# Moving weight-block loads, factors and stores to other steps of the first four attention jobs

## The chip, the cores and the metric

One core of a Trainium2 chip. The metric is the device time in microseconds of one execution; lower is better. TensorE (PE in the profile) does the matmuls, ScalarE (ACT) exponentials and copies, VectorE (DVE) sums and reductions. SyncE (SP) issues most DMAs, GpSimd (POOL) issues the accumulating ones.

## The reference

Two attention layers over x of shape (8, 512, 32, 32), fp32. For each batch element and layer, with S = 1024 positions, C = 512 channels and 8 heads of 64:

```python
xn  = groupnorm(x, 8 groups) * gamma + beta
q, k, v = Wq xn + bq, Wk xn + bk, Wv xn + bv        # 512 x 512 weights
out = softmax(q^T k / 8) v                          # per head, over 1024 positions
x   = x + Wp out + bp
```

## The kernel before, in words

The 16 pairs of batch element and layer are jobs, numbered n = 0 to 15 and ordered so that two batch elements go through layer 0 (jobs 0 and 1) and then through layer 1 (jobs 2 and 3), and so on. For each job TensorE runs the projections and then the attention.

**Projections** are done by Strassen-like recipes with seven products in place of eight. They need sums of weight blocks ("factors"). One level of this needs the seven sums of a whole matrix (S1 to S4 beside the raw blocks); two levels need seven such sets, 49 small blocks, stored as seven tiles of 128 x 7 x 128. The weights are the same for all batch elements, so the sums are made once, in jobs 0 to 3, and kept in DRAM: `keep` (one level) or `deep_...` tiles. Later jobs fetch these with `fetch()` (line 181) into a ring of six tiles; the profile names the transfer w<-deep.

The sums are made on VectorE in the attention of the early jobs, beside TensorE's work, by two helpers:

- `put_round(which, layer)` makes all 49 blocks of one matrix ("a round" or batch): a load of four raw blocks (round<-wp_dram or round<-wqkv_dram, 256 KB each), eight chores of VectorE (`first` and `second`, lines 165 to 171, four of 128x512 and four of 128x896), and seven stores of 448 KB (deep<-round). Jobs 0 to 3 do the output matrix of layer 0, V of layer 1, output of layer 1, V of layer 0.
- `put_first(which, layer)`, in jobs 0 and 1 only, makes the one-level factors of K and of Q of layer 1: a load (raw<-wqkv_dram, four of 256 KB), four chores (128x512), and a store in two DMAs, 768 and 256 KB (keep<-raw).

Both take the same SBUF buffer, tag "deep", of which there is one. The inner sums of the next job's activations (`deep_steps`, lines 485 to 491) are written to it as well. Each user waits until the one before is stored or read. In job 0 the order is round, raw, deep; in job 1 raw, round, deep; in jobs 2 and 3 round, deep.

**Attention** of a job is 64 steps i, in eight groups g (four head pairs by two halves of the queries). A step does the scores sc of one block of keys on TensorE, the exponential e on ScalarE (line 1107), and the product with the values (po) for step i - 2. The sums of e per query are made by VectorE (acc, lines 1121 and 1123), partly by GpSimd's accumulating DMA e<-e (line 1130) and an add of its result (line 1133). Each group ends with a take of po into q (line 1176) and a reduction of acc (line 1188, called at step 8g + 10). After an odd g the reciprocals follow: `gather` (three small DMAs r<-r, line 1211), `invert` (line 1215 on, then the DMA rd<-rt and two broadcasts back, rb<-rd, lines 1228 and 1230), `normalise` (line 1245, q times rb). Their times after the reduction are written down:

```python
times = (0.0, 12.0, 12.1, 22.0) if n in ROUNDS and g < 4 else (0.0, 7.6, 7.7, 16.2)
```

A step advances the planner's clock by 1.71, the end of a group by another 0.85. So in jobs 0 to 3 the first inversion (g = 1, reduced in step 18) comes within step 25, ahead of that step's tables, and its multiply at the end of step 30; the second (g = 3, reduced in step 34) comes within step 41, and its multiply at the end of step 46.

**Order.** PE, ACT and DVE run in the order in which the program is written. What is done beside attention stands in three tables by step, called at the end of the step in this order: `chores` (VectorE's work, at most one a step: `put` takes the next free step), `moves` (loads, stores, ScalarE's work, likewise by `move`), `leaving` (a round's stores, two per step). DMAs of `in_turn` keep their place in SP's program. SP starts them one after another, and an entry that waits holds all behind it.

In the kernel before, the tables come to these steps:

| | job 0 | job 1 | jobs 2, 3 |
|---|---|---|---|
| round: load | 6 | 12 | 9 |
| round: eight chores | 12-16, 18-20 | 16, 18, 22-27 | 13-16, 18-21 |
| round: stores | 27-30 | 28-31 | 27-30 |
| raw: load | 35 | 2 | |
| raw: four chores | 39-42 | 6, 7, 9, 10 | |
| raw: store | 43 | 11 | |
| sums of the next job's xn (t, lines 426 to 432) | 31-34 | 17, 19-21 | 31-34 |
| inner sums into "deep" | 46-49 | 37-40, 42, 44, 46, 48 | 36-38, 40, 41, 43, 45, 47 |

The groupnorm of the next job but one stands beside this: in job 1 its `groups` (DMAs dg and mr) at step 8, its coefficients at 14, its four applies on ScalarE at 15 to 18.

Of the kernel before, what the change touches and what calls it, by code (L numbers as in the profile page):

```python
# [54 lines left out]
ROUNDS = {0: (O, 0), 1: (V, 1), 2: (O, 1), 3: (V, 0)}  # L55
# [26 lines left out]
def fast_path(  # L82
# [33 lines left out]
    def later(delay, fn):  # L116
        todo.append((clock[0] + delay, fn))
# [97 lines left out]
    def deep_round(which, layer):  # L215


        box = []

        def start():  # L220
            t = acts.tile([P, NW, NW, P], F32, tag="deep", name=f"round_{which}_{layer}")
            box.append(t)
            for i in range(2):
                for j in range(2):
                    in_turn(
                        t[:, 2 * j + i, 0:4, :].rearrange("p (cc h) o -> p cc (h o)", cc=2),
                        raw_block(layer, which, i, j),
                    )

        def outer_(part):  # L230
            factor(box[0][:, :, 0:4, :], part)

        def inner(part):
            factor(box[0].rearrange("p f a o -> p a f o"), part)

        def store(o):
            keep = wdram.tile([P, NW, P], F32, name=f"deep_{which}_{layer}_{o}")
            in_turn(keep, box[0][:, FACTOR[o]])
            deep[which, layer, o] = keep

        first = [lambda part=part: outer_(part) for part in range(4)]
        second = [lambda part=part: inner(part) for part in range(4)]
        return start, first, second, [lambda o=o: store(o) for o in OUTER]
# [1186 lines left out]
    first = v_phase(0, (1, 5, 2, 6, 7, 3, 4), v0)  # L1430
# [113 lines left out]
    for n in range(-1, len(jobs)):  # L1544
        last = n + 1 == len(jobs)
        outs = None
        if n >= 0:
            chores, moves, leaving = {}, {}, {}

            def put(i, fn):  # L1550
                while i in chores:
                    i += 1
                chores[i] = fn
                return i

            def move(i, fn):
                while i in moves:
                    i += 1
                moves[i] = fn
                return i  # L1560

            def put_round(which, layer):
                load, first, second, stores = deep_round(which, layer)
                begin = {0: 6, 1: 12}.get(n, 9)
                move(begin, load)
                at = begin + 3
                for fn in first:
                    at = put(at + 1, fn)
                for fn in second:
                    at = put(at + 1, fn)  # L1570
                at = max(at, 26)
                for i in range(4):
                    leaving[at + 1 + i] = lambda part=stores[2 * i : 2 * i + 2]: [fn() for fn in part]

            def put_first(which, layer):
                at = move(35 if n == 0 else 2, lambda: start()) + 3
                box = []

                def start():
                    box.append(acts.tile([P, NW, 2, CH], F32, tag="deep", name=f"raw_{n}"))  # L1580
                    load_blocks(box[0], layer, which)

                for part in range(4):
                    at = put(at + 1, lambda part=part: factor(box[0], part))
                move(at + 1, lambda: store_factors(box[0], layer, which))

            if last:
                w = last_weights(n)
                for part in range(4):
                    put(12 + 2 * part, lambda part=part: factor(w, part))  # L1590
                for i, fn in enumerate(last_sums(0)):
                    put(49 + 3 * i, fn)
            else:
                for i, (_, fn) in enumerate(extra):
                    put(2 + i, fn)
                if n == 1:
                    at = (8, 14, 15, 16, 17, 18, 17, 19, 20, 21)
                else:
                    for i, fn in zip((3, 3, 4, 5, 5, 6, 7, 7, 8), reads):
                        put(i, fn)  # L1600
                    at = (16, 22, 23, 24, 26, 27, 29, 31, 33, 35)
                    if n < DEEP_V + 2:
                        at = (17, 24, 26, 27, 29, 30, 31, 32, 33, 34)
                for i, fn in zip(at[:2], steps):
                    put(i, fn)
                for i, fn in zip(at[2:], steps[2:]):
                    move(i, fn)
                if n == 1:
                    put_first(*FIRST[n])
                for i, fn in zip(at[len(steps) :], sums(n + 1)):  # L1610
                    put(i, fn)
                if n in ROUNDS:
                    put_round(*ROUNDS[n])
                if n == 0:
                    put_first(*FIRST[n])
                put(52 if n in ROUNDS else 48, lambda q=att.q: out_combine(q, None, 0))
                deep_first = deep_steps(n + 1)
                if n + 1 >= DEEP_V:
                    for i, fn in enumerate(deep_first):
                        put(37 + 2 * i if n not in ROUNDS else ((37, 38, 39, 40, 42, 44, 46, 48) if n == 1 else (36, 37, 38, 40, 41, 43, 45, 47))[i], fn)  # L1620
                else:
                    for at, fn in zip((46, 47, 48, 49), deep_first[4:]):
                        put(at, fn)
                move(58, lambda: extend_plan(n + 1))
                for _ in range(RING):
                    move(58, fetch)
            assert max([*chores, *moves], default=0) < NT * len(att.groups) + LEAD
            if n + 1 >= DEEP_V and not last:
                outs = OutputSums(n)
                ahead = deque()  # L1630
                if jobs[n][1] == 1 and jobs[n][0] + 2 < B:
                    ahead.extend(load_steps(jobs[n][0] + 2))
                both, plan_sums = deep_phases(n + 1, ahead, outs)

                att.run(chores, moves, leaving, True)
                extra = ahead
                plan_sums()
                banks(0, "one")
                if n + 2 < len(jobs):
                    reads, steps = norm_steps(n + 2)  # L1640
                att.take(len(att.groups) - 1, both[0])
                banks(1, "one")
                for thunk in both[1:]:
                    thunk()
                banks(0, "two")
                att = Attention(n + 1)
                att.scores(0)
                att.scores(1)
                banks(1, "two")
                att.scores(2, "po")  # L1650
                continue
            att.run(chores, moves, leaving)
            banks(0, "one")
            banks(1, "one")
            if last:
                for i, fn in enumerate(last_sums(1)):
                    later(7.1 + 0.8 * i, fn)
                later(13.0, judge)
                for sh in range(2):
                    last_proj(n, w, sh)  # L1660
                break
            outs = OutputSums(n)
            out_sums(n, outs)
            first = v_phase(n + 1, ORDER)
            for thunk in first[:-1]:
                thunk()
            rest = first[-1:]
            extra = deque()
            if jobs[n][1] == 1 and jobs[n][0] + 2 < B:
                extra.extend(load_steps(jobs[n][0] + 2))  # L1670
            if n == 0:
                load, bias_steps = make_out_bias(1)
                extra.append((8, load))
                extra.extend((11, fn) for fn in bias_steps)
            if n + 2 < len(jobs):
                reads, steps = norm_steps(n + 2)
                if n + 2 <= DEEP_V:
                    extra.extend((15, fn) for fn in reads)
        both, _ = deep_phases(n + 1, extra, outs, deep_first[:4] if outs else ())
        both[0]()  # L1680
        rest[0]()
        if n < 0:
            later(22.0, lambda: load_x(1))
        for thunk in both[1:]:
            thunk()
        banks(0, "two")
        att = Attention(n + 1)
        att.scores(0)
        att.scores(1)
        banks(1, "two")  # L1690
        att.scores(2, "po")
# [249 lines left out]
```

## Time and profile before

| | |
|---|---|
| median of 3 runs | 3171.83 us (3170.29 to 3174.29) |
| the profiled execution | 3173.06 us, span 3171.3 us |
| TensorE clock granted, mean | 0.998 |
| first scores of jobs 0, 1, 2, 3 | 78.86, 285.10, 487.48, 683.18 us |
| DMA moved | 450.31 MB, mean 142 GB/s |

Times in views are microseconds from the start of the span. In a list of waits, each line names the engine, the line and the result of the operation that waited, what it waited for, and then the total, the number of waits and the longest. A line of a timeline gives start, duration, engine, line, operation, operands and, in brackets, the idle time before it and what ended that. SPq is SP's queue of issues: its durations are those of issuing, not of moving data.

### The profile page before, as it was taken

What the parts mean: (1) busy time and instruction counts of PE and PEld (TensorE: products, weight loads), DVE (VectorE), ACT (ScalarE), POOL (GpSimd) and SP (SyncE); (2) the same over time, 40 slices, a digit from 0 to 9 for tenths busy, and PEclk for the clock granted to TensorE, in tenths of its full rate; (3) what the DMA queues carried; (4) which work ended last, traced back from release to release, by engine and by line L of the source; (5) the groups of instructions that cost most, each with busy time, mean ns of one, the idle gap of its engine ahead of it and who ended that gap; (6) DMA issues with size and microseconds to landing.
All of it is one profiled execution on the core that took longest, in us unless ns stands there. A gap on an engine that the chain in (4) does not pass through costs nothing.

```text
span 3171.3 us, 62173 instructions
## 1 busy us (share of the span) xinstructions
PE 3151.6 (99%) x24093; PEld 1874.4 (59%) x24093; DVE 2636.1 (83%) x3571; ACT 2333.4 (74%) x4233; POOL 281.1 (9%) x318
## 2 busy tenths in 40 slices
PE   9999999999999999999999999999999999999999
PEld 7356384663946639366483754837557375573844
DVE  8887898979879788896978969789697887978967
ACT  6648687786877768677686776867768687686864
POOL 0100101001010010100001000010000100001000
PEclk9999999999999999999999999999999999999999
DMA  7645575566635454455554535446456463444733
GB/s 277 149 132 164 136 225 134 145 190 153 219 75 148 109 141 137 85 163 148 141 179 95 163 91 142 120 95 188 129 138 181 89 202 62 132 126 95 223 75 82
DMA packets 186190, 450.31 MB, mean 142 GB/s; under 512 B 37928, under 2 KB 54176, under 8 KB 185888
## 3 DMA queue, kind: packets, MB, share of 16 engines
q1 hardware_dynamic: 137040, 296.82, 27.3%
q0 software_dynamic: 48848, 149.44, 25.9%
q8 instruction: 192, 3.15, 0.4%
q14 instruction: 110, 0.90, 0.1%
HBM read 247.41 MB, written 48.17 MB: 93 GB/s over the span
## 4 chain that ended last, share of the span: by engine, by line
PE 92%; DVE 4%; DMA 1%; issue 1%; SPq 0%; ACT 0%; DVEq 0%; POOL 0%; ACTq 0%; POOLq 0%
PE sc L1102 25%; PE po L1153 25%; PE vd L809 11%; PE zd L809 11%; PE yd L809 5%; PE ud L809 4%; PE vd L804 4%; PE zd L804 3%; PE ud L804 1%; PE yd L804 1%; DVE acc L1123 1%; PE z L556 1%; DVE acc L1133 1%; DMA keep<-raw 0%; DVE r L1188 0%
## 5 line engine op out<-in xcount | busy, mean ns | idle before, releaser
L1107 ACT ACTIVATE e<-sc 128x1024 f32<-128x1024 f32 x1024 | 1044.4, 1025 | 573.9 <-PE sc L1102 546.7
L1153 PE MATMUL po<-e,v 64*64 64x512 f32 x8192 | 1057.7, 589 | 2.0 <-ACT e L1107 2.0
L1102 PE MATMUL sc<-q,k 64*64 64x512 f32 x8192 | 1058.2, 589 | 0.3 <-ACT e L1107 0.2
L1153 PEld LDWEIGHTS po<-e,v 64*64 64x64 f32 x8192 | 312.9, 133 | 568.5 <-issue 541.3
L1102 PEld LDWEIGHTS sc<-q,k 64*64 64x64 f32 x8192 | 311.0, 133 | 563.7 <-issue 508.6
L1123 DVE TENSOR_TENSOR acc<-acc,e 128x1024 f32<-128x1024 f32 x320 | 389.7, 1218 | 39.3 <-ACT e L1107 28.6
L1130 POOL DMA_DIRECT2D e<-e x224 | 192.9, 861 | 1759.5 <-ACT e L1107 1297.9
L1121 DVE TENSOR_TENSOR acc<-e,e 128x1024 f32<-128x1024 f32 x128 | 156.5, 1223 | 147.6 <-ACT e L1107 147.5
L1133 DVE TENSOR_TENSOR acc<-acc,e 128x1024 f32<-128x1024 f32 x224 | 272.6, 1217 | 1.8
L809 PE MATMUL zd<-deep,w 128*128 128x256 f32 x860 | 240.1, 379 | 0.0
L809 PE MATMUL vd<-deep,w 128*128 128x256 f32 x804 | 223.5, 379 | 0.0
L809 PEld LDWEIGHTS zd<-deep,w 128*128 128x128 f32 x860 | 163.4, 190 | 22.2
L809 PEld LDWEIGHTS vd<-deep,w 128*128 128x128 f32 x804 | 152.8, 190 | 20.8
L1188 DVE TRANSPOSE_TENSOR_REDUCE r<-acc 128x32 f32<-128x1024 f32 x128 | 159.4, 1245 | 4.3
L904 POOL DMA_DIRECT2D x<-p x61 | 72.9, 1196 | 972.2 <-ACT p L826 510.3
L851 DVE TENSOR_TENSOR p<-p,s 128x512 f32<-128x512 f32 x185 | 127.5, 689 | 23.8 <-ACT p L826 19.4
L804 PE MATMUL vd<-w,deep 128*128 128x128 f32 x840 | 119.5, 276 | 1.5 <-ACT ud L504 1.5
L851 DVE TENSOR_TENSOR q<-q,s 128x512 f32<-128x512 f32 x64 | 44.2, 691 | 87.3 <-ACT q L828 45.6
L804 PEld LDWEIGHTS vd<-w,deep 128*128 128x128 f32 x840 | 106.5, 192 | 2.0 <-ACT ud L504 1.9
L804 PE MATMUL zd<-w,deep 128*128 128x128 f32 x728 | 106.9, 276 | 0.1
L809 PE MATMUL vd<-os,w 128*128 128x256 f32 x364 | 105.5, 379 | 0.0
L809 PE MATMUL zd<-os,w 128*128 128x256 f32 x356 | 98.9, 379 | 0.0
(296 smaller groups left out, 4824.6 us busy)
## 6 DMA issues: line engine op xcount, KB each, us to landing
w<-deep SPq DMA_DIRECT2D x399, 448.0 KB, 4.9
e<-e POOLq DMA_DIRECT2D x224, 512.0 KB, 4.7
x<-p POOLq DMA_DIRECT2D x61, 512.0 KB, 6.7
rb<-rd SPq DMA_DIRECT2D x96, 256.0 KB, 3.7
x<-x_dram SPq DMA_DIRECT2D x28, 512.0 KB, 5.5
out_dram<-x SPq DMA_DIRECT2D x28, 512.0 KB, 5.5
deep<-w SPq DMA_DIRECT2D x28, 448.0 KB, 5.9
deep<-round SPq DMA_DIRECT2D x28, 448.0 KB, 9.4
```

The source lines that it names most:

```text
L804: nc.tensor.matmul(ps[:, tokens], moving[i][:, tokens], lhs[:, FACTOR[i], :], start=(start and ti == 0), stop=True, skip_group_check=True,)
L809: nc.tensor.matmul(ps, lhs[:, FACTOR[i], :], moving[i], start=start, stop=True, skip_group_check=True,)
L851: nc.vector.tensor_add(to_, to_, five.to_broadcast([P, 2, QT]))
L904: nc.gpsimd.dma_start(to_, p(part), accum_op=ALU.add)
L1102: nc.tensor.matmul(sc[h * HD : (h + 1) * HD, j, :], k[r, hp, k0 : k0 + HD], q[r, hp, sh * HALF : (sh + 1) * HALF], start=True, stop=True,)
L1107: nc.scalar.activation(e, sc, AF.Exp, scale=SCALE)
L1121: nc.vector.tensor_add(acc[g], self.es[i - 1], e)
L1123: nc.vector.tensor_add(acc[g], acc[g], e)
L1130: nc.gpsimd.dma_start(self.summed[i], self.summed.pop(i - 1), accum_op=ALU.add)
L1133: nc.vector.tensor_add(self.acc[g], self.acc[g], self.summed.pop(i))
L1153: nc.tensor.matmul(po[g][j * HD : (j + 1) * HD, h, :], v[r, kc, d0 : d0 + HD], e[r, j, :], start=(kc == 0), stop=(kc == NT - 1),)
L1188: nc.vector.tensor_reduce(self.r[:, 0, m, :], self.acc.pop(g).rearrange("p j (b e) -> p (j b) e", e=RP), AX.X, ALU.add, apply_transpose=True,)
```

## The change

It moves work to other steps; no operation is added or taken out.

- Job 0: the round's stores follow its last chore. The raw blocks' load is asked for at step 29 in place of 35 (29 and 30 are taken by applies, so it comes to 31), their chores start from a fixed step, and the inner sums come two steps sooner.
- Job 1: the raw chores follow directly on the load; the round's load moves from 12 to 8, its chores stand in a row, its stores follow; the sums of xn come after them; the inner sums come two steps sooner.
- Jobs 2 and 3: the stores follow the last chore.

```diff
             def put_round(which, layer):
                 load, first, second, stores = deep_round(which, layer)
-                begin = {0: 6, 1: 12}.get(n, 9)
+                begin, at = {0: (6, 11), 1: (8, 14)}.get(n, (9, 12))
                 move(begin, load)
-                at = begin + 3
-                for fn in first:
+                for fn in first + second:
                     at = put(at + 1, fn)
-                for fn in second:
-                    at = put(at + 1, fn)
-                at = max(at, 26)
                 for i in range(4):
                     leaving[at + 1 + i] = lambda part=stores[2 * i : 2 * i + 2]: [fn() for fn in part]
 
             def put_first(which, layer):
-                at = move(35 if n == 0 else 2, lambda: start()) + 3
+                at = {0: 35, 1: 2}[n]
+                move({0: 29, 1: 2}[n], lambda: start())
                 box = []
...
                 if n == 1:
-                    at = (8, 14, 15, 16, 17, 18, 17, 19, 20, 21)
+                    at = (8, 14, 15, 16, 17, 18, 23, 24, 25, 26)
                 else:
...
-                        put(37 + 2 * i if n not in ROUNDS else ((37, 38, 39, 40, 42, 44, 46, 48) if n == 1 else (36, 37, 38, 40, 41, 43, 45, 47))[i], fn)
+                        put(37 + 2 * i if n not in ROUNDS else ((35, 36, 37, 38, 40, 42, 44, 46) if n == 1 else (36, 37, 38, 40, 41, 43, 45, 47))[i], fn)
                 else:
-                    for at, fn in zip((46, 47, 48, 49), deep_first[4:]):
+                    for at, fn in zip((44, 45, 46, 47), deep_first[4:]):
                         put(at, fn)
```

The tables after it:

| | job 0 | job 1 | jobs 2, 3 |
|---|---|---|---|
| round: load | 6 | 8 | 9 |
| round: eight chores | 12-16, 18-20 | 15-22 | 13-16, 18-21 |
| round: stores | 21-24 | 23-26 | 22-25 |
| raw: load | 31 | 2 | |
| raw: four chores | 36-39 | 3-6 | |
| raw: store | 40 | 7 | |
| sums of the next job's xn | 31-34 | 23-26 | 31-34 |
| inner sums into "deep" | 44-47 | 35-38, 40, 42, 44, 46 | 36-38, 40, 41, 43, 45, 47 |

## The prediction

> **What bounds the kernel now.** I read the page first. TensorE is busy almost without a break:
>
> ```profile
> PE 3151.6 (99%) x24093; PEld 1874.4 (59%) x24093; DVE 2636.1 (83%) x3571; ACT 2333.4 (74%) x4233; POOL 281.1 (9%) x318
> ```
>
> Only some 20 us of the 3171.3 us span are not matmul, so the question is whether the edited stages hold part of them. The edits touch attention jobs 0 to 3. Their first scores start at 78.86, 285.10, 487.48 and 683.18 us by the timeline. Second view, TensorE's waits from 79 to 485 us (engine, line and operation, what it waited for, total, times, longest):
>
> ```profile
> PE v L556 <- DVE q L1176: 3.5, 1, 3.5
> PE vd L804 <- DMA w<-deep: 2.3, 1, 2.3
> PE po L1153 <- ACT e L1107: 2.0, 2, 1.7
> PE z L556 <- DMA w<-wqkv_dram: 1.2, 1, 1.2
> PE vd L804 <- ACT ud L504: 1.1, 1, 1.1
> PE sc L1102 <- ACT e L1107: 0.2, 1, 0.2
> ```
>
> The timeline places them. Job 0 loses 1.74 at 187.5, 1.21 at 190.3 and 3.48 at 197.2: 6.43 us. Job 1 loses 0.28 at 394.5, 2.31 at 395.9, 1.1 at 415.3 and about 0.7 near 318. Later stages show next to nothing (0.42 at 807.9). Third, stretches of time (length, busy time of PE, PEld, DVE, ACT, POOL, granted clock, DMA share, GB/s):
>
> ```profile
> 200.00:204.00 4.00, 2.96 (x7) 2.43 (x8) 3.83 (x9) 0.00 (x0) 0.00 (x0) 0.57 0.84 259
> ...
> 396.00:400.00 4.00, 1.69 (x13) 1.28 (x7) 3.97 (x4) 0.59 (x1) 0.00 (x0) 0.81 1.02 365
> 400.00:404.00 4.00, 4.00 (x29) 4.00 (x29) 3.69 (x4) 2.97 (x8) 0.00 (x0) 0.76 1.02 404
> ```
>
> After each group of waits the clock falls: 4 x 0.43 = 1.72 us lost in job 0, 4 x (0.19 + 0.24) = 1.72 in job 1. The neighbours stand at 1.00.
>
> Why is TensorE late only there? The waits end on VectorE, or on weight fetches that queue behind VectorE's work. VectorE's own waits, first of 79 to 200, then of 285 to 400 us:
>
> ```profile
> DVE deep L485 <- DMA keep<-raw: 5.9, 1, 5.9
> DVE raw L165 <- DMA raw<-wqkv_dram: 4.9, 1, 4.9
> ```
>
> ```profile
> DVE deep L485 <- issue: 5.9, 1, 5.9
> ...
> DVE round L165 <- DMA round<-wqkv_dram: 5.7, 1, 5.7
> ```
>
> So VectorE stands 10.8 us in job 0 and 11.6 in job 1 for weight blocks in the one "deep" buffer. (The third, called issue, ends when the seven stores deep<-round have landed: the last was issued at 348.73.) After each stall it runs unbroken to the end of the job, so it cannot catch up. The last column sum of the attention shows the debt:
>
> ```profile
> 200.90 1.24 DVE L1188 TRANSPOSE_TENSOR_REDUCE r<-acc 128x32 f32<-128x1024 f32 x1
> ```
>
> ```profile
> 601.47 1.25 DVE L1188 TRANSPOSE_TENSOR_REDUCE r<-acc 128x32 f32<-128x1024 f32 x1
> ```
>
> The first is 122.0 us after job 0's first score, the second 114.0 after job 2's; job 1 has 120.8, job 3 114.7. Jobs 2 and 3 run without those TensorE waits, so 8.0 and 6.8 us of lateness is what has to go.
>
> Last, SP's issues (start, length of issue):
>
> ```profile
> 115.34 1.85 SPq L1211 DMA_DIRECT2D r<-r  x3
> 124.93 0.33 SPq L1228 DMA_DIRECT2D rd<-rt  x1
> 126.31 1.31 SPq L1230 DMA_DIRECT2D rb<-rd  x2
> 127.67 8.71 SPq L155 DMA_DIRECT2D deep<-round  x7
> 143.57 2.55 SPq L1211 DMA_DIRECT2D r<-r  x3
> 146.31 3.22 SPq L155 DMA_DIRECT2D raw<-wqkv_dram  x4
> ```
>
> SP issues in program order. The raw loads of job 0 stand behind the second r<-r, which waits for VectorE's reduction at 142.3; the stores stand behind rd/rb, although their data was finished at 115.9.
>
> **What the Trainium skill says.** "TensorE: Matmul & The Clock Gate", What's actually happening: an idle window of about 3.4 us halves TensorE's clock, and a busy one restores it. The trace agrees: two spells of 3.413 us at 0.5, after these two groups of waits; but job 1's 2.6 us of standing were enough for it. The same page, Architectural detail: VectorE's queue is strictly first in, first out. The trace agrees: during the 5.89 us stand, adds whose operands were ready stood behind it. "DMA: Bandwidth & Descriptors", HWDGE ordering: descriptors of one queue are taken in order, and a transfer's completion lands only after the earlier writes of the same DMA engines. So rd placed behind stores lands after them. The trace agrees in kind: rd landed 1.4 us after its issue on quiet engines (124.93), 4.8 after (157.78) with accumulations under way.
>
> **The change, part by part.** No instruction is added or removed; all durations below are of this trace. Steps are 1.717 us apart.
>
> *Job 0, stores* (steps 27-30 to 21-24). The inversion with rd/rb runs inside step 25, so all seven stores now precede it on SP. They start behind r<-r at 117.2 rather than 127.7. Issuing seven took 6.7 us in job 1 and 8.7 here, so SP is free at 124 to 126; rt is ready at 124.9, so rd slips by 0 to 1 us. Data: 448 KB per 1.12 us in the steady part, 7.8 us in all, plus 1 to 2 for the accumulation still running until about 119.5: drained at 128 to 129.5. The engines stood idle in 120:124 (share 0.02), so this cover exists. rd lands at about 129.5 rather than 126.3, rb follows at 129.5 to 131 and lands at 134 to 136 (133.6 before). VectorE waits for it at L1245: 0.5 to 2.5 us instead of 1.2. I take +1.
>
> *Job 0, raw blocks* (step 35 to 31; 29 and 30 are taken). They now stand before the step-34 r<-r, directly after rb: issue 131 to 133, landing after 4.9 us at 136 to 138. Their first factor comes to VectorE at 144.7. Cover 7 us: the wait of 4.87 goes. Queued behind them on SP is r<-r, not ready until 143.5, so it loses nothing.
>
> *Job 0, their store and the next "deep" sums* (factors 39-42 to 36-39, store 43 to 40, sums 46-49 to 44-47). From 144.65 + 1, four factors of net 0.61 and three adds (3.6) end at 151.8. The store is now before the second rd on SP (invert at step 41), lands after 5.9 (its time before): 157.7. Until its first deep sum VectorE has two pair adds, a take, an inversion and a reduction: 1.14 + 0.61 + 1.66 + 2.35 = 5.8, so 157.6. The wait of 5.89 becomes 0 to 1.8; I take 0.5. The second rb comes later than this store by SP's order, but its multiply is only at the end of step 46: covered to within 1 us.
>
> Sum: 10.8 - 1.5 = 9.3 us earlier, against 8.0 needed. The take that TensorE's v waited for ended 122.1 after the first score, and TensorE without earlier waits wants it at about 114.9: 112.8 suffices, with 2.1 to spare. Gain 6.43 + 1.72 = 8.15; I subtract 0.8 for stalls above that cover.
>
> *Job 1, raw factors* (6,7,9,10 to 3-6; store 11 to 7). The loads landed at about 291 (packets), and VectorE is free at 290.5 and stood 3.6 us for the first exponentials; two factors (1.2) fit there for nothing. The last ends at 297.9 rather than 305.8, the store lands some 5 to 7.6 us later: 303 to 305.5.
>
> *Job 1, the round* (load 12 to 8, factors from 16-27 to 15-22, stores 28-31 to 23-26). dg and mr, ready at 302, still go first; the load follows at 304.7 to 306, landing in 5.7: 310.4 to 312. The first factor is reached at 312.5: the wait of 5.71 becomes 0 to 1. The sums of xn move to 23-26, after their applies at 15-18; nobody reads them before step 35. VectorE's work in steps 15 to 26 is 8 us per eight steps of attention plus 7.0 of factors, 4.5 of sums and 1.7 of inversion, about 25 in 20.6 us: 4 us late at step 26, as job 2 is. Four stores precede rd, three follow rb. Stores at 326 to 337, the last lands by 344 to 346, deep sums (37 to 35) at about 347: the wait of 5.9 becomes 0 to 1. Removed about 10, needed 6.8, so job 1 should take job 2's period: 202.38 - 195.70 = 6.68 us gained (the direct losses and the clock add to 6.1).
>
> *Jobs 2 and 3*: only the stores move, 27-30 to 22-25, six ahead of rd. Same arithmetic: rb 1 to 2 us later, VectorE waiting 0 to 2 more. Job 1's fetch landed at 113.0 and cost 2.3; job 2's landed by about 106: a slack of 5 covers it. Gain from the earlier buffer 1.3 at L485 in one stage, off TensorE's path. I take 0.5 lost for both, bounds -0.4 to +2.
>
> Total: -8.15 + 0.8 - 6.68 + 0.5 = -13.5. Against the profiled execution (3173.06 us, span 3171.3) that is 3159.5; it stood 1.2 above the median 3171.83 of three runs, which gives **3158.3**.
>
> **The rivals.** (a) Forecast, both ends clear: 3156 to 3161, chance 0.70. (b) One of the two stages pays: rb's late landing or the raw store still holds VectorE 4 us or more in it. The 2.1 us of spare in job 0 speak for it. Then -6.7 to -8.2: 3164 to 3166, 0.15. (c) Slower: the store burst drains at half that rate, because accumulations share the engines (154 GB/s in 116:120). Then 16 us of draining put rd at 135, rb at 140 and VectorE 7 us at L1245 in each of four stages. Jobs 0 and 1 then gain nothing, jobs 2 and 3 overrun their slack of 5 by 2 and pay the clock's 1.7: +7.4, 3179. It decides from an rb some 6 us later than now. Against it: 369 GB/s in 140:144, mostly these stores. 0.08. (d) SP's order does not follow the new places, or other delays eat the gain: 3168 to 3173, 0.07.
>
> **The numbers.** 0.2% is 6.3 us, about what a measurement of this kernel can tell from no change. Faster: (a) and most of (b), 0.82. Same: the rest of (b) and (d), 0.10. Slower: (c), 0.08. The range 3155.5 to 3167 holds (a) with run spread and (b).
>
> **What would show it.** Right: no TensorE wait over 1 us from 79 to 485, clock 1.00 there, job 0 to job 1 in 198 us (206.2), job 1 to 2 in 195.7; no VectorE wait for raw or round; last reductions at 113 to 115. Wrong: a wait of VectorE at L1245 for rb over 5 us, or TensorE's v still waiting for the take.

## The result, and the profile after

The changed kernel takes 3165.73 us (median of 16 runs, 3164.14 to 3168.74) against 3172.49 us of the kernel before, measured beside it: ratio 0.9979, 95% interval 0.9971 to 0.9986, about 6.8 us less. The forecast of the size was -13.5 us. The profiled execution has a span of 3163.9 us, 7.4 less than before.

The first scores of successive jobs give the account. A period is the time from one job's first score to the next one's.

| | before | after | difference | forecast |
|---|---|---|---|---|
| first score of job 0 | 78.86 | 79.39 | +0.5 | 0 |
| period of job 0 | 206.24 | 202.98 | -3.3 | -7.35 |
| period of job 1 | 202.38 | 196.30 | -6.1 | -6.7 |
| periods of jobs 2 and 3 | 195.70, 196.25 | 197.12, 196.15 | +1.3 | +0.5 |

Job 1 paid, job 0 paid less than half, job 2 lost a little. TensorE's waits from 79 to 485 us, as before in the order engine, line and operation, what it waited for, total, times, longest:

```profile
PE v L556 <- DVE q L1176: 3.3, 1, 3.3
PE sc L1102 <- ACT e L1107: 0.2, 1, 0.2
```

Four of the six lines are gone and a small one stays, but the largest wait, v for the take at the end of job 0, stands nearly as it was (3.3 of 3.5 us). The clock follows it (same columns as in the prediction's stretches):

```profile
196.00:200.00 4.00, 1.84 (x4) 1.51 (x5) 3.80 (x8) 0.00 (x0) 0.00 (x0) 0.74 0.84 277
200.00:204.00 4.00, 4.00 (x17) 3.39 (x16) 3.84 (x11) 1.11 (x2) 0.00 (x0) 0.83 0.78 273
396.00:400.00 4.00, 4.00 (x38) 4.00 (x37) 3.78 (x12) 3.30 (x10) 0.00 (x0) 1.00 0.64 170
400.00:404.00 4.00, 4.00 (x38) 4.00 (x38) 3.93 (x6) 3.30 (x10) 0.00 (x0) 1.00 0.25 96
```

Job 1's spell of half clock is gone, job 0's costs 4 x (0.26 + 0.17) = 1.7 us as before. VectorE's waits in job 0 (79 to 205 us) say why:

```profile
DVE q L1245 <- DMA rb<-rd: 8.7, 2, 5.3
...
DVE deep L485 <- DMA keep<-raw: 0.4, 1, 0.4
```

The waits for raw (4.9) and keep (5.9) went as forecast, to 0 and 0.4. In their place VectorE stands 8.7 us for the reciprocals. In the kernel before, the same list had

```profile
DVE q L1245 <- DMA rb<-rd: 1.2, 1, 1.2
```

SP's issues of the same stretch:

```profile
117.78 7.83 SPq L155 DMA_DIRECT2D deep<-round  x7
125.72 1.03 SPq L1228 DMA_DIRECT2D rd<-rt  x1
130.49 1.45 SPq L1230 DMA_DIRECT2D rb<-rd  x2
132.12 3.19 SPq L155 DMA_DIRECT2D raw<-wqkv_dram  x4
148.23 2.11 SPq L1211 DMA_DIRECT2D r<-r  x3
155.14 1.47 SPq L155 DMA_DIRECT2D keep<-raw  x2
158.29 0.33 SPq L1228 DMA_DIRECT2D rd<-rt  x1
164.67 1.31 SPq L1230 DMA_DIRECT2D rb<-rd  x2
```

rb is issued when rd has landed. The first rd takes 4.8 us behind the seven stores (1.4 before), the second 6.4 us behind keep (4.8 before). VectorE's first stand, in its timeline, ends when rb lands at 138.2:

```profile
138.28 1.23 DVE L1245 TENSOR_TENSOR q<-q,rb 128x1024 f32<-128x1024 f32 x1 [5.30 <-DMA rb<-rd]
```

### The profile page after: what moved, and what is told of

Read it like the earlier page. It is cut to its first block, busy times and chain, and to the rows that moved or that the text cites. A ratio compares the mean times of both kernels' runs of the same rounds, so it can differ in the third digit from the quotient of the medians.

```text
span 3163.9 us, 62177 instructions
## 1 busy us (share of the span) xinstructions
PE 3151.1 (100%) x24093; PEld 1874.2 (59%) x24093; DVE 2637.1 (83%) x3571; ACT 2333.1 (74%) x4233; POOL 281.0 (9%) x318
## 4 chain that ended last, share of the span: by engine, by line
PE 98%; DVE 1%; ACT 0%; issue 0%; DMA 0%; SPq 0%; DVEq 0%; ACTq 0%
PE sc L1102 28%; PE po L1153 27%; PE vd L809 11%; PE zd L809 11%; PE yd L809 5%; PE ud L809 4%; PE vd L804 4%; PE zd L804 3%; PE ud L804 1%; PE yd L804 1%; PE z L556 1%; DVE acc L1123 1%; PE z_last L1045 0%; PE v L556 0%; PE y L556 0%
```

## The experiments

Theory A: what job 0 and job 2 still lose is VectorE standing at L1245 for rb, because rd now stands behind the stores. Rivals: VectorE simply has too much work in job 0 (B); rb is late because of other transfers and not because of the order on SP (C, later E and F); the place of the multiply alone is what counts (D). Ratios are to the kernel before, run beside each.

**The multiply later.** In the changed kernel:

```diff
-            times = (0.0, 12.0, 12.1, 22.0) if n in ROUNDS and g < 4 else ...
+            times = (0.0, 12.0, 12.1, 28.0) if n in ROUNDS and g < 4 else ...
```

> The changed kernel with the multiply of L1245 for the first two pairs of jobs 0 to 3 at 28.0 in place of 22.0 us after its reduction, so at the end of step 33 (49) in place of 30 (46); no DMA moves. Theory A: what is left in job 0 (TensorE's v waits 3.3 us for the take, and the clock spell of 1.7) comes from VectorE standing 5.3 + 3.4 us at L1245 for rb; with other work drawn ahead of it, both waits fall under 1 us, job 0's last reduction comes at 113 to 115 us after its first score (118.6 now), v's wait goes, job 0's period falls from 202.98 to about 198, job 2's from 197.1 to 195.7: in all 6 us less than the changed kernel, near 3159.5. Theory B: VectorE has too much work in job 0 whether it stands or not: the last reduction stays over 117 and under 1.5 us is gained.

Measured: 3161.07 us, ratio 0.9957 (0.9943 to 0.9971). TensorE's only wait from 79 to 485 us:

```profile
PE sc L1102 <- ACT e L1107: 0.2, 1, 0.2
```

Job 0's period is 197.85, job 2's 195.57, job 3's 195.87; the last reduction of job 0 comes 111.9 us after its first score, and no half clock follows. With not one DMA moved, v's wait is gone: A holds, B falls.

**The stores of job 0 late again.** In the changed kernel:

```diff
                 for fn in first + second:
                     at = put(at + 1, fn)
+                if n == 0:
+                    at = 26
```

> The changed kernel with only job 0's seven round stores back at steps 27-30, behind the first rd and rb. Theory A (the stores ahead of rd are what made rb late): the first wait at L1245 in job 0 falls from 5.3 to about 1.2 us, the second (3.4) stays, the raw loads come some 4 us later on SP and their first factor waits 0 to 3 us; on balance 1 to 4 us of standing go, v waits 0 to 2.5 us, 1 to 4 us less than the changed kernel. Theory C (rb is late because the accumulations or the raw loads share the DMA engines, wherever the stores stand): the first wait stays over 4 us and the time is that of the changed kernel or 1 to 3 us more.

Measured: 3168.86 us, ratio 0.9983 (0.9976 to 0.9991); period of job 0 204.08. The first wait at L1245 fell as A said, but the balance was wrong. VectorE's waits in job 0:

```profile
DVE raw L165 <- DMA raw<-wqkv_dram: 8.5, 1, 8.5
...
DVE q L1245 <- DMA rb<-rd: 1.4, 2, 1.2
...
DVE deep L485 <- DMA keep<-raw: 1.2, 1, 1.2
```

TensorE's v does not wait here, but z waits 2.3 us for w<-wqkv_dram, and 6.83 us at half clock follow, so job 0 is no shorter than in the changed kernel.

The raw load needs the "deep" buffer, so it waits on SP until the stores have landed: issued at 145.1 in place of 132.1. The early stores are what makes the early raw load possible; the two have to be judged together.

**The stores of jobs 2 and 3 late again.** As above with `if n > 1:`.

> The changed kernel with the round stores of jobs 2 and 3 back at steps 27-30. Theory A: job 2's wait at L1245 goes from 3.5 to 1.2 us and the two TensorE waits of 0.2 and 0.8 us after job 2's attention go, period 195.7 in place of 197.1; job 3 unchanged; 1.4 us less than the changed kernel. A rival (the 1.4 us are scatter of one execution): no difference in the period.

Measured: 3167.28 us, ratio 0.9975 (0.9965 to 0.9985), which can't be told from the changed kernel. In the profile job 2's period is 195.57 in place of 197.12 and its waits of 0.2 and 0.8 us are gone, as A says. Job 0, which was not edited, took 204.04 in this execution: its two stands at L1245 summed to 10.2 us.

**Job 1's part alone**, in the kernel before:

```diff
-                begin = {0: 6, 1: 12}.get(n, 9)
+                begin = {0: 6, 1: 8}.get(n, 9)
...
-                at = begin + 3
+                at = 14 if n == 1 else begin + 3
...
-                at = max(at, 26)
+                if n != 1:
+                    at = max(at, 26)
...
-                at = move(35 if n == 0 else 2, lambda: start()) + 3
+                at = move(35 if n == 0 else 2, lambda: start()) + (3 if n == 0 else 0)
...
-                    at = (8, 14, 15, 16, 17, 18, 17, 19, 20, 21)
+                    at = (8, 14, 15, 16, 17, 18, 23, 24, 25, 26)
...
-                        put(... ((37, 38, 39, 40, 42, 44, 46, 48) if n == 1 else ...
+                        put(... ((35, 36, 37, 38, 40, 42, 44, 46) if n == 1 else ...
```

> The kernel before with job 1's part of the change alone (raw factors at 3-6, round's load at 8, factors 15-22, stores 23-26, sums 23-26, inner sums from 35). If the parts add: job 1's period falls from 202.4 to 196.3 us, all else as before, so 6.1 us less than the kernel before, about 3166. Rival: job 1's gain leans on job 0 ending sooner, and alone it gives under 3 us.

Measured: 3169.12 us, ratio 0.9985 (0.9978 to 0.9992). Job 1's period is 196.31, job 0's 206.53: the part gives its 6.1 us in the profile without job 0's. The runs show 4.6 us (2.5 to 7.0 by the interval).

**The multiply later in the kernel before**, the first edit and nothing else.

> The kernel before with the multiply of L1245 at 28.0 in place of 22.0 us in jobs 0 to 3, and nothing else. Theory A: it takes away only the 1.2 us at L1245; the waits for raw (4.9) and keep (5.9) in job 0, and for round (5.7) and the stores (5.9) in job 1, stay, so job 0 and job 1 keep periods within 1.5 us of 206.2 and 202.4: 0 to 3 us less than the kernel before. Rival D (the place of the multiply is what counts, the moves of the change add little): most of the 13 us come with it.

Measured: 3175.30 us, ratio 1.0003 (0.9995 to 1.0011). Waits for raw 5.6, keep 5.5, round 6.0 and the stores 5.0 us stay; periods 206.75 and 200.66, the second 1.7 us under the kernel before where at most 1.5 was expected. D falls: moving the multiply gains nothing that these runs can tell while the waits for blocks stand.

**Only the first multiply later, only the second.** In the changed kernel `28.0 if g < 2 else 22.0`, and `22.0 if g < 2 else 28.0`.

> The changed kernel with the multiply of only the first pair (g = 1) at 28.0. Theory A: the wait of 5.3 us goes, the second (3.4) stays or shrinks to 1, since the second rd is then issued ahead of the next accumulation, as in the run with both later; last reduction of job 0 by 113.5, so no wait of v: job 0's period about 198, 5 us less than the changed kernel. Theory B (each us of standing counts, with no spare): 3.4 us of standing still leave v late by 0.5 to 2 us.

> The changed kernel with the multiply of only the second pair (g = 3) at 28.0. The first wait of about 5.3 us stays, the second goes; last reduction of job 0 near 115.2 in place of 118.6, and TensorE wants the take at about 115: v waits 0 to 1 us, with or without the clock spell of 1.7. So 3 to 5 us less than the changed kernel by theory A; a wait of v over 2 us would say that the second standing was not on the path.

Measured: 3161.07 us, ratio 0.9956 (0.9941 to 0.9972), and 3163.85 us, ratio 0.9966 (0.9954 to 0.9978). With only the first moved, the second stand shrinks to 1.5 us and v does not wait. With only the second moved, the first stays at 5.3, the last reduction comes at 116.4, v waits 1.1 us without a spell of half clock, and a product of the projections that follow (zd, line 809) waits 1.9 us for a copy by ScalarE, which itself stood 2.8 us for the DMA x<-p. So of the 3.5 us by which job 0's period (201.35) exceeds that with the first multiply moved (197.85), 1.1 are v's wait, and the 1.9 are not traced to L1245. The first stand is still the larger cause, and it makes most of the second: without it keep's store is issued 71.3 us after the first score in place of 75.8, and rd lands 1.4 us after its issue:

```profile
151.07 0.82 SPq L155 DMA_DIRECT2D keep<-raw  x2
154.22 0.33 SPq L1228 DMA_DIRECT2D rd<-rt  x1
155.60 2.09 SPq L1230 DMA_DIRECT2D rb<-rd  x2
```

**The raw load late again**, the stores early. In the changed kernel:

```diff
-                move({0: 29, 1: 2}[n], lambda: start())
+                move({0: 35, 1: 2}[n], lambda: start())
```

> The changed kernel with job 0's raw load asked for at step 35 again, behind the second r<-r on SP; the stores stay ahead. It tells what made rb land 7.7 us after its issue. Theory E (the raw loads issued right behind rb share the engines with it): the first wait at L1245 falls from 5.3 to 3.5 us or less. Theory F (the accumulation e<-e issued before rb is in front of it): the wait stays within 0.7 us of 5.3. By both, the raw load is then issued near 148 us and its first factor waits 2 to 4 us, so the kernel loses 1 to 4 us against the changed one.

Measured: 3169.94 us, ratio 0.9988 (0.9979 to 0.9996). VectorE's waits in job 0:

```profile
DVE raw L165 <- DMA raw<-wqkv_dram: 7.0, 1, 7.0
DVE q L1245 <- DMA rb<-rd: 5.8, 1, 5.8
```

With nothing issued behind rb until 148.7, the first wait is 5.8 us: E falls. The raw factor then waits 7.0 us, more than expected, and job 0's period is 207.17: early stores alone gain nothing in job 0.

**No accumulations beside rb.** In the changed kernel, for one group of job 0:

```diff
-            return 0 if g + 1 == len(self.groups) else 2
+            return 0 if g + 1 == len(self.groups) or (self.n == 0 and g == 3) else 2
```

> The changed kernel where the fourth group (g = 3) of job 0 alone sums its first four exponentials on VectorE instead of with two accumulating DMAs; these two are the ones issued at 126.5 and 130.0 us, around rd and rb. Theory F (they are what rb waits behind): rd lands in under 3 us (4.8 now) and rb within 4 us of its issue (7.7 now), so the first wait at L1245 falls from 5.3 to 2 us or less, though VectorE has two more adds in the group (2.4 us). If instead something else holds rb, the wait stays over 4 us. The time tells little here, since the adds take most of the gain.

Measured in a single execution of each kernel: 3162.97 us beside 3172.63. Job 0's period is 199.37 us, 3.6 less than in the changed kernel, so the adds took less of the gain than expected. rd was issued at 126.52 and still took 4.4 us, so it waits for the stores and not for the accumulations; that half of F falls. rb landed at 135.9, 5.0 us after its first issue in place of 7.7:

```profile
130.89 1.32 SPq L1230 DMA_DIRECT2D rb<-rd  x2
135.91 1.23 DVE L1245 TENSOR_TENSOR q<-q,rb 128x1024 f32<-128x1024 f32 x1 [0.54 <-DMA rb<-rd]
```

VectorE's waits, where the wait for keep is new, since this edit also brings the second inversion ahead of keep's store:

```profile
DVE deep L485 <- DMA keep<-raw: 6.6, 1, 6.6
...
DVE q L1245 <- DMA rb<-rd: 0.5, 1, 0.5
```

The stand at L1245 is not a clean test, since VectorE came to it later by its added work; rb's landing is the better sign. By it 2.7 of rb's 7.7 us belong to the accumulations, on one execution's evidence.

## Why the prediction was right or wrong

**Right: what bounds.** Lateness of VectorE from waits on the "deep" buffer cost TensorE its waits and two half-clock spells. With the stands at L1245 gone too (first experiment), the time falls by 0.43%, 13.6 us by ratio, which is the gain forecast for the change, but in another kernel.

**Right: job 1.** Its waits of 5.7 and 5.9 us became 0.8 and none, keep's store was issued 12.7 us after the job's first score (forecast 12.8) and the round's load 19.1 us after it (forecast 19.6 to 20.9). The gain of 6.1 is under 6.68 because the 0.7 us near its steps 19 and 20 stayed. The direct sum of 6.1 hit the figure partly by luck: it counted these 0.7 us, and without them it is 5.4; where the other 0.7 came from isn't shown.

**Wrong: job 0's first rb.** The step "rb follows at 129.5 to 131 and lands at 134 to 136" failed. Job 0 began 0.53 us later in this execution, which is taken off here. The drain of the stores was right (forecast 128 to 129.5; their last packet ends at 129.4), rd landed at 130.0 where 129.5 was forecast. But rb was given 4.5 to 5 us of travel, although it had taken 7.3 us in the kernel before (126.31 to 133.6). The stores behind it did not make that length: in that trace rb's packets run from 129.0 to 132.7 us, and the first packet of the stores starts at 132.3. In the changed kernel rb took 7.7 us with no stores behind it, and it was as late with nothing behind it at all (the run with the raw load late). 2.7 us of that went with the accumulations in the last run.

The order of issue tells more (times here as they stand in the traces). In the changed kernel GpSimd issues the two accumulations at

```profile
126.53 0.87 POOL L1130 DMA_DIRECT2D e<-e  x1 [9.42 <-DMA deep<-round]
129.97 0.87 POOL L1130 DMA_DIRECT2D e<-e  x1 [2.56 <-ACT e L1107]
```

In the kernel before they came at 126.0 and 129.4, and rb (126.31) was issued ahead of the second, whose packets start at 134.2, after rb's last. In the changed kernel rb (130.49) comes behind both: their packets run from 128.4 to 135.6, and rb's first packet starts only at 133.5. No run moved rb past the second accumulation alone, so this part is read from the traces and not tested.

So the slip of 3.7 us in rd's landing passed whole to rb, which landed at 137.7: 4.1 us more of standing, where 1 was taken. The prediction's own landing of 134 to 136 meant a stand of 1.6 to 3.6 us and not the 0.5 to 2.5 beside it, since VectorE came to L1245 at 132.4 in the kernel before; against the 1.2 of before that is 0.4 to 2.4 us more, so the +1 taken was low rather than out of place. (The times that the prediction gives for TensorE's waits are up to 0.6 us early; their lengths are right.)

**Wrong: job 0's second rb.** "Covered to within 1 us" was 3.4. It followed from the first: keep's store was issued 2.8 us later than forecast (154.6 against 151.8, the 0.53 taken off), and the rd behind it took 6.4 us with an accumulation under way, 1.4 us where keep came sooner. In the sum this stand was put at nothing. Together the two took back 7.5 of the 10.4 us removed, and the last reduction came 3.4 us sooner (122.0 to 118.6 us after the first score) instead of 9.3. The limit for v was well placed: 114.9 forecast, 115.5 by the changed kernel's trace (v is wanted at 194.9, the first score is at 79.4). The failed term is the standing at L1245, 2.2 us in the sum and 8.7 in the trace, against 2.1 us of spare.

**Jobs 2 and 3.** The added standing, 2.3 and 1.2 us at the first rb, lay in the bounds of 0 to 2 or just over them. Job 2's slack of 5 us was computed for the fetch; the products after it waited 1.0 us nonetheless, and its period grew by 1.4 where 0.5 was taken for both jobs.

**The rivals.** (b), one stage pays, is what happened, with its figure of 3164 to 3166. (c) named the mechanism, a wait at L1245 in place of the one removed, and put it 7 us long; its place and kind were right. Its cause was not, since the stores drained in the time forecast, nor was its reach: in job 1 the longest stand was 1.3 us.

## What to carry to other kernels

When a transfer is moved ahead of a small one that an in-order engine reads back, price the small one's whole round trip from its own rows in the trace, and don't put its length down to a neighbour that the trace doesn't separate. Look also at what other queues issue between its old and its new moment. The consumer of the late transfer can sometimes be moved behind ready work; here a multiply six microseconds later gave what the earlier store had taken back. The same shift gained nothing in the kernel before, where longer waits on the same engine stood beside it.

## What the runs showed of the hardware

A wait of TensorE of 3.3 us brought 3.41 us at half clock, from 197.94 us in the changed kernel, as the wait ended; so did two waits of 2.6 us in sum (job 1 of the kernel before) and two of 1.8 us in sum at the end of job 0 (the run with the raw load late). Single waits of 1.1 and 1.9 us (the run with only the second multiply later) did not, nor did two of 1.74 and 1.21 us at 188.1 and 190.9 us in the kernel before. So the sum of the waits doesn't decide by itself; what does, these runs don't show. The start differs from one execution to the next: the first score came between 78.86 and 80.72 us, so up to 1.9 us between two profiled spans can come from the start alone.
